# A four-layer graph network in float32: the second-last batch, too, mirrors a quarter of its symmetric products through VectorE and HBM, under a new instruction plan

## The chip, the cores and the metric

The kernel runs on one NeuronCore of a Trainium2 chip. The metric is the device time of one execution in microseconds (us). Before the change it is 2437.61 us, the median of three runs (2435.33 to 2437.78). The profile is that of one further execution, with a span of 2440.0 us.

The engines are named as in the profile: PE is TensorE's matrix multiplication and PEld its loading of weights, DVE is VectorE, ACT is ScalarE, POOL is GpSimd, SP is SyncE, from whose queue most transfers start.

## The reference, cut to what matters

There are 16 batches. Each has 1024 nodes with 128 features (`x`) and a 1024 x 1024 matrix of edge weights (`adj`), and passes four layers, each of the form x = x + layer(relu(layernorm(x))). All is float32. Two of the layers hold products that are symmetric in their two node indices, and the change is about these.

```python
# layer 0: three convolutions, each with a symmetric 1024 x 1024 product
def _adapt_conv(h, edge_weight, W, b, is_last):
    h = h @ W + b
    nh = h / jnp.maximum(jnp.linalg.norm(h, axis=-1, keepdims=True), EPS)
    cos = jnp.einsum('bij,bkj->bik', nh, nh)          # symmetric
    h = jnp.einsum('bpq,bqc->bpc', edge_weight * cos, h)
    return h if is_last else jax.nn.relu(h)

# layer 1: x_agg = adj^T x, then two dense layers         [cut]
# layer 2: attention over the edges, tanh and softmax     [cut]

# layer 3: one more symmetric product
    h = jnp.einsum('bnf,of->bno', x, W_w) + W_b
    e = jnp.einsum('bil,bkl->bik', h @ A, h)
    e = e + jnp.swapaxes(e, 1, 2)                       # symmetric
    att = jax.nn.softmax(jnp.where(adj > 0, e, 0), axis=1) * adj
    h_prime = jax.nn.relu(jnp.einsum('bij,bjk->bik', att, h))
    # ... gates and output                                [cut]
```

So a batch has four symmetric products: three in layer 0 and one in layer 3.

## The kernel before

The 1024 nodes are eight blocks of 128, so a product is an 8 x 8 grid of 128 x 128 blocks. It is made row by row (`j`), each row in two halves (`s`) of four blocks, that is 512 columns, one PSUM bank. Only the blocks on and above the diagonal are multiplied out (36 of 64). The 28 below it are mirrored from the blocks above, which are kept in SBUF in a buffer named `above`. There are two ways to mirror a block.

- **By TensorE.** ACT copies the blocks right of the diagonal from PSUM to `above`; later TensorE transposes each into the PSUM bank of its row.
- **By VectorE and HBM** (`by_dma`), for the lower left quarter only: rows 4 to 7, left half. VectorE transposes the right halves of rows 0 to 3 in squares of 32 x 32 as it takes them from PSUM to `above`; a transfer stores two rows of them to HBM, and four transfers bring them back with the squares in their mirrored places, into a buffer named `got`. VectorE then reads the half row from `got` in SBUF instead of from PSUM.

```python
def far(b, product):                       # which batches use VectorE and HBM
    return (b > 0 or "v" in FLAGS and product > 0) and b < (B - 1 if "u" in FLAGS else B - 2)

class Square:
    def row(self, j, s):
        lo, hi = HALVES[s]                                     # (0, 4), (4, 8)
        if self.by_dma and j >= QUARTER and s == 0:            # QUARTER is 4
            q = j - QUARTER
            return self.got, lambda: self.got.t.rearrange("p (r c d) -> p c r d", r=QUARTER, d=P)[:, q]
        dst = ps(f"sq_{self.k}_{j}_{s}")
        first = max(lo, j)
        if first < hi:
            pe(...)      # L761: one matmul of the blocks from the diagonal on
        n = min(hi, j) - lo
        if n > 0:
            pe(...)      # L771: n transposes of kept blocks, 128 x 128 each
        return dst, lambda: by_block(dst.t, D, 4)

    def keep(self, j, s, read):
        lo, hi = HALVES[s]
        if self.by_dma and j < QUARTER and s == 1:
            dve(...)     # L783: nc.vector.transpose of the four blocks, in squares
            if j % 2:
                self.send(j - 1, j + 1)    # L803 one store, L814 four loads
            return
        first = max(lo, j + 1)
        if first < hi:
            act(...)     # L793: nc.scalar.copy of the blocks right of the diagonal
    # [send() cut: one transfer above -> by_hbm, four by_hbm -> got]
```

Layer 0 uses a row like this, layer 3 in the same way with `e` and `hs` in place of `ew` and `h`:

```python
square = Square(k, hTn, hTn, "abc"[i] in FLAGS and far(b, i))
for j in range(NB):
    ew = chunk(f"ew_{k}_{j}")
    for s, (lo, hi) in enumerate(HALVES):
        pc, view = square.row(j, s)
        square.keep(j, s, pc)
        dve(...)         # L960: ew = (product * rn) * adjT, half a row
    accumulate(acc, h, j, D, ew, j)          # L823 (L834 in the last convolution)
```

With the flags of the kernel before, batches 1 to 13 mirror the quarter through HBM, and batches 0, 14 and 15 mirror all by TensorE.

The order of the instructions is not that of the program text. Each instruction is an `Op` with an assumed duration; `Plan.order()` lays all of them out on the engines in assumed time and then issues them in that order. Among the instructions that could start now, it takes the one of lowest rank:

```python
lead = self.leads.get(o.key + o.edge, self.leads.get(o.key, 0.0))
o.rank = (self.deadline(o.batch) - o.tail - lead, o.seq)
# deadline: lambda b: min(b * PERIOD, (B - 2) * PERIOD + LAST)
# o.tail: the longest chain of assumed durations behind it
```

`LEADS` has a number for each kind of instruction, with separate ones for the first two batches (`<0`, `<1`) and the last two (`>1`, `>0`). `KINDS` tells for each kind of buffer the pool, how many may be held at once, and how many by batches younger than the oldest in work. Two or three batches are in work at a time. The plan decides only order and buffers; the engines wait on semaphores as the data demand.

Of the kernel before, what the change touches and what calls it, by code (L numbers as in the profile page):

```python
# [222 lines left out]
def tile_adj_preln(  # L223
# [38 lines left out]
    hbm = ctx.enter_context(tc.tile_pool(name="hbm", bufs=1, space=bass.MemoryType.DRAM))  # L262
# [28 lines left out]
    FLAGS = set("CabcdkxhyzT")  # L291
# [34 lines left out]
    for load_it in first:  # L326
# [11 lines left out]
    POOLS = {"adjT": 16, "adjL": 5, "x": 3, "big": 13, "above": 2, "got": 1, "bank": 8, "small": 29, "row": 6, "hbm": 3, "hrow": 2}  # L338
    KINDS = {
        "adjT": ("adjT", 16, 16), "adjL": ("adjL", 5, 5), "x": ("x", 3, 3), "w4": ("big", 12, 8),  # L340
        "chunk": ("big", 11, 4), "above": ("above", 2, 1), "got": ("got", 1, 1), "ps": ("bank", 5, 5),
        "acc": ("bank", 8, 6), "small": ("small", 7, 6), "row": ("row", 3, 3), "hbm": ("hbm", 3, 2),
        "hrow": ("hrow", 2, 1),
    }
    PERIOD, LAST, AHEAD, WINDOW = 60.0, 52.0, 2, 0.05

    LEADS = {
        "0 ACT hT": -1, "0 DVE hn": -8, "0 DVE mv": 42.5, "0 DVE nb": -20, "0 DVE st": -77.5, "0 PE ps": -72.5,
        "0 POOL rstd": -1, "00 ACT above": -10.5, "00 ACT hT": 95, "00 ACT hTn": -20.5, "00 ACT sq": -31,
        "00 DMA by": -13.5, "00 DMA got": 15.5, "00 DVE above": -135, "00 DVE ew": 79.5, "00 DVE h": -95.5,  # L350
        "00 DVE ss": -131.5, "00 PE acc0": -252.5, "00 PE ps": -142, "00 PE psP": -0.5, "00 PE sq": -18.5,
        "00 POOL rn": -129.5, "01 ACT above": 56, "01 ACT hT": 11.5, "01 ACT hTn": 15, "01 ACT sq": 15.5,
        "01 DMA by": 4.5, "01 DMA got": 18.5, "01 DVE above": 4.5, "01 DVE ew": 51.5, "01 DVE h": -2.5,
        "01 DVE ss": 16, "01 PE acc0": -164.5, "01 PE ps": 42, "01 PE psP": -5.5, "01 PE sq": -11,
        "02 ACT above": -2, "02 ACT hTn": -615, "02 ACT sq": -25.5, "02 DMA by": 63.5, "02 DMA got": 0.5,
        "02 DVE above": 43.5, "02 DVE ew": -232.5, "02 DVE ss": 79.5, "02 DVE x": -55.5, "02 PE acc0": -28.5,
        "02 PE ps": 12.5, "02 PE sq": 222, "02 POOL rn": -103, "1 ACT g": -33, "1 ACT hn": 66, "1 ACT y1": -7.5,
        "1 DMA adjL": -113, "1 DVE adjL": -21, "1 DVE hn": 1.5, "1 DVE mv": 237.5, "1 DVE nb": 46,
        "1 DVE st": -625.5, "1 DVE x": -0.5, "1 PE acc1": 4, "1 PE py": -167.5, "1 PE py2": 67,
        "1 POOL rstd": -43, "2 ACT e2": -24, "2 ACT h": 287.5, "2 ACT hfl": 53, "2 ACT hn": -13.5,  # L360
        "2 ACT hnT": 18, "2 ACT s1": -14, "2 DVE alone": -51.5, "2 DVE e2": 48.5, "2 DVE h": 20,
        "2 DVE hn": 48.5, "2 DVE hrow": -43.5, "2 DVE mv": -2.5, "2 DVE nb": 78, "2 DVE rden": 9.5,
        "2 DVE x": 10, "2 PE acc2": 108.5, "2 PE p1": -90, "2 PE pf": -26.5, "2 PE ps": 117.5, "2 PE psP": -315,
        "2 POOL rstd": 4.5, "3 ACT above": -19.5, "3 ACT e3": 96.5, "3 ACT gate": -185.5, "3 ACT h3T": 19.5,
        "3 ACT hn": -84.5, "3 ACT hnT": -9.5, "3 ACT hp": -5, "3 ACT hpT": 41, "3 ACT hs": 46.5, "3 ACT z": 25,
        "3 DMA by": -13.5, "3 DMA got": 0.5, "3 DMA z": -130.5, "3 DVE e3": -363.5, "3 DVE gate": 83,
        "3 DVE h": -111.5, "3 DVE hn": 69, "3 DVE mv": -2, "3 DVE nb": 147, "3 DVE st": -192, "3 DVE sum": 53.5,
        "3 DVE top": -84, "3 DVE z": -925, "3 PE acc3": -130.5, "3 PE pg": -18.5, "3 PE ps": 19,
        "3 PE psN": 114, "3 PE psP": 95, "3 PE sq": -0.5, "3 POOL rstd": -59, "3 POOL z": 0.5,
        "T ACT adjT": 1.5, "T DMA adjT": -140.5, "T DVE adjT": -391, "x DMA x": 54.5, "0 ACT hT <0": -2,  # L370
        "0 ACT hT >1": -4.5, "0 ACT hn <1": -4.5, "0 DVE hn <0": 8.5, "0 DVE hn <1": 8.5, "0 DVE hn >0": 15.5,
        "0 DVE hn >1": 1, "0 DVE mv <0": -4.5, "0 DVE mv <1": 113, "0 DVE mv >0": 47.5, "0 DVE mv >1": -25.5,
        "0 DVE nb <0": 101.5, "0 DVE nb <1": -62.5, "0 DVE nb >0": -49, "0 DVE nb >1": -18.5,
        "0 DVE st <0": -85, "0 DVE st <1": -73.5, "0 DVE st >0": -122.5, "0 DVE st >1": -32, "0 PE ps <0": 85.5,
        "0 PE ps <1": 36, "0 PE ps >0": -31, "0 PE ps >1": 40, "0 POOL rstd <0": -6.5, "0 POOL rstd <1": -26,
        "0 POOL rstd >0": -7, "0 POOL rstd >1": 15.5, "00 ACT above <0": -32, "00 ACT above <1": -88,
        "00 ACT above >0": -294, "00 ACT above >1": -3, "00 ACT hT <0": 147.5, "00 ACT hT <1": -7,
        "00 ACT hT >0": 21, "00 ACT hT >1": 161.5, "00 ACT hTn <0": -70.5, "00 ACT hTn <1": 119.5,
        "00 ACT hTn >0": -22, "00 ACT hTn >1": -11, "00 ACT params <0": -26, "00 ACT sq <0": -34,
        "00 ACT sq <1": 134.5, "00 ACT sq >0": -119, "00 ACT sq >1": -25.5, "00 DMA by <1": 0,  # L380
        "00 DMA got <1": 1, "00 DVE above <1": -197, "00 DVE ew <0": 180, "00 DVE ew <1": 13,
        "00 DVE ew >0": -125, "00 DVE ew >1": -147.5, "00 DVE h <0": -25.5, "00 DVE h <1": -4.5,
        "00 DVE h >0": 12, "00 DVE h >1": -50.5, "00 DVE params <0": 171, "00 DVE ss <0": 0,
        "00 DVE ss <1": -73.5, "00 DVE ss >0": -46.5, "00 DVE ss >1": -4, "00 PE acc0 <0": -39.5,
        "00 PE acc0 <1": -212, "00 PE acc0 >0": -327.5, "00 PE acc0 >1": -253.5, "00 PE params <0": 56.5,
        "00 PE ps <0": -18.5, "00 PE ps <1": -16, "00 PE ps >0": -32, "00 PE ps >1": -130.5,
        "00 PE psP <0": -2.5, "00 PE psP <1": 32, "00 PE psP >0": -22.5, "00 PE psP >1": -43,
        "00 PE sq <0": 28.5, "00 PE sq <1": 10, "00 PE sq >0": 3.5, "00 PE sq >1": 10, "00 POOL rn <0": -11,
        "00 POOL rn <1": -164.5, "00 POOL rn >0": -96.5, "00 POOL rn >1": -144, "01 ACT above <0": 113,
        "01 ACT above <1": -11, "01 ACT above >0": 65.5, "01 ACT above >1": 24, "01 ACT hT <0": -15,  # L390
        "01 ACT hT <1": -17.5, "01 ACT hT >0": 3.5, "01 ACT hT >1": -39, "01 ACT hTn <0": 16.5,
        "01 ACT hTn <1": -22, "01 ACT hTn >0": 68, "01 ACT hTn >1": 8, "01 ACT sq <0": 174,
        "01 ACT sq <1": -3.5, "01 ACT sq >0": -69, "01 ACT sq >1": 107, "01 DMA by <1": -9, "01 DMA got <1": 25,
        "01 DVE above <1": -5, "01 DVE ew <0": 140, "01 DVE ew <1": -13.5, "01 DVE ew >0": -9.5,
# [983 lines left out]
    params = Buf(None, [], "params")  # L1378
# [57 lines left out]
```

## Time and profile before

| | before |
|---|---|
| time, median of three | 2437.61 us |
| span of the profiled execution | 2440.0 us |
| PE busy | 2389.2 us (98%) |
| DVE busy | 2106.2 us (86%) |
| ACT busy | 1288.3 us (53%) |
| POOL busy | 230.9 us (9%) |
| mean granted TensorE clock | 0.995 |
| HBM read, written | 198.14 MB, 62.91 MB |

Busy time is the time in which an engine executed at least one instruction; the shares are of the span. A float32 product appears in the records as two matmul records, a transpose by TensorE as one. Matmuls are pipelined: the recorded end of one lies behind the start of the next, so the distance from start to start is the better measure of what one costs. A line such as L771 is the place in the kernel that issued the instruction; the names beside it are the program's buffers, with the numbers left out (`sq<-ident,above` is a mirrored block, `got<-by_hbm` the load of squares). "Us to landing" of a transfer counts from its issue until its data are there.

### The profile page before, as it was taken

To read this page: it belongs to the slowest core of one execution; us is meant where nothing else is said; L and a number is where in the kernel's file an instruction comes from. 1 tells how busy PE (TensorE), PEld (TensorE's weight loads), DVE (VectorE), ACT (ScalarE), POOL (GpSimd) and SP (SyncE) were. 2 spreads that over 40 slices of the span, in tenths; PEclk is the share of its full clock that TensorE was granted. 3 is DMA by queue.
4 is the path that set the end of the run, shared out by engine and by line. 5 is a ranking of instruction groups with operands and counts; after the bars stand their busy time and mean duration, and the time that the engine had idled before them with its cause. 6 is when DMAs were issued, how large, how long until landed. Compare 5 with 4: busy or idle time off the path is not lost. (4 is left out here: it accounts for less than half of the span.)

```text
span 2440.0 us, 34840 instructions
## 1 busy us (share of the span) xinstructions
PE 2389.2 (98%) x11946; PEld 1588.9 (65%) x11946; DVE 2106.2 (86%) x5264; ACT 1288.3 (53%) x2404; POOL 230.9 (9%) x141
## 2 busy tenths in 40 slices
PE   6999999999999999999999999999999999999996
PEld 3568576675766757576575766757676575765763
DVE  5767989888998988999889998999989888897677
ACT  4425564644646455454644646455454655656275
POOL 1100010100101001011010100101011010101021
PEclk9999999999999999999999999999999999999999
DMA  8632837559296583946739296493946738054000
GB/s 127 131 96 43 147 78 139 126 93 178 54 160 132 85 158 78 159 109 114 160 75 182 58 153 134 87 162 68 162 116 105 164 78 156 18 87 95 25 2 18
DMA packets 1129473, 263.35 MB, mean 108 GB/s; under 512 B 971856, under 2 KB 1112912, under 8 KB 1129296
## 3 DMA queue, kind: packets, MB, share of 16 engines
q1 hardware_dynamic: 1108368, 251.73, 54.9%
q10 hardware_dynamic: 20928, 9.40, 1.4%
q8 instruction: 94, 1.54, 0.3%
q14 instruction: 83, 0.68, 0.1%
HBM read 198.14 MB, written 62.91 MB: 107 GB/s over the span
## 5 line engine op out<-in xcount | busy, mean ns | idle before, releaser
L960 DVE SCALAR_TENSOR_TENSOR ew<-sq,rn,adjT 128x512 f32<-128x512 f32 x612 | 432.0, 738 | 72.1 <-ACT above L793 37.4
L823 PE MATMUL acc<-ew,h 128*128 128x512 f32 x1024 | 481.5, 597 | 3.6 <-DVE ew L960 3.6
L761 PE MATMUL sq<-hTn 128*128 128x512 f32 (+3 forms) x1152 | 431.4, 487 | 0.3 <-ACT hTn L623 0.3
L793 ACT COPY above<-sq 128x256 f32<-128x256 f32 (+3 forms) x432 | 167.8, 393 | 439.0 <-PE sq L761 239.7
L761 PEld LDWEIGHTS sq<-hTn 128*128 128x128 f32 x1152 | 200.9, 191 | 153.2 <-issue 103.5
L823 PEld LDWEIGHTS acc<-ew,h 128*128 128x128 f32 x1024 | 179.8, 192 | 164.1 <-issue 124.1
L834 PEld LDWEIGHTS acc<-h,ew 128*128 128x128 f32 x2048 | 240.7, 192 | 23.0 <-issue 17.3
L834 PE MATMUL acc<-h,ew 128*128 128x128 f32 x2048 | 250.3, 276 | 0.0
L823 PE MATMUL acc<-e,hs 128*128 128x512 f32 x512 | 242.5, 598 | 5.6 <-DVE e L1203 4.4
L834 PEld LDWEIGHTS acc<-h,e 128*128 128x128 f32 x2048 | 232.9, 192 | 11.9 <-issue 6.5
L834 PE MATMUL acc<-h,e 128*128 128x129 f32 x2048 | 233.8, 275 | 1.2 <-DVE e L1110 1.2
L823 PE MATMUL acc<-adjL,hn 128*128 128x512 f32 x512 | 233.4, 593 | 0.3 <-ACT hn L727 0.3
L563 POOL TENSOR_TENSOR rstd<-ve,mhalf 128x8 f32<-128x8 f32 x64 | 105.1, 1642 | 1249.7 <-DVE ve L682 1197.6
L1194 ACT ACTIVATE e<-e,top 128x1024 f32<-128x1024 f32 x128 | 147.0, 1149 | 135.8 <-DVE top L1190 134.4
L771 PEld LDWEIGHTS sq<-ident,above 128*128 128x128 f32 x960 | 125.8, 141 | 135.4 <-issue 89.9
L891 ACT ACTIVATE adjT<-adjT 128x1024 f32<-128x1024 f32 x128 | 135.1, 1056 | 146.0 <-DVE adjT L888 109.4
L771 PE MATMUL sq<-ident,above 128*128 128x128 f32 x960 | 175.7, 274 | 9.7 <-ACT above L793 9.7
L888 DVE STREAM_TRANSPOSE adjT<-adjT 128x1024 f32<-128x1024 f32 x128 | 155.0, 1224 | 28.2 <-DMA adjT<-in_adj_dram 21.6
L706 ACT ACTIVATE hn<-x,nb,rstd 128x128 f32<-128x128 f32 x256 | 105.3, 483 | 123.6 <-DVE nb L690 117.8
L1110 DVE SCALAR_TENSOR_TENSOR e<-adjT,e 128x512 f32<-128x512 f32 x256 | 158.7, 679 | 9.3 <-ACT e L1106 8.8
L783 DVE STREAM_TRANSPOSE above<-sq 128x512 f32<-128x512 f32 x208 | 146.5, 706 | 17.2 <-PE sq L761 17.2
L1203 DVE TENSOR_TENSOR e<-e,adjT 128x512 f32<-128x512 f32 x248 | 161.0, 680 | 0.0
(130 smaller groups left out, 3493.8 us busy)
## 6 DMA issues: line engine op xcount, KB each, us to landing
adjT<-in_adj_dram SPq DMA_DIRECT2D x512, 128.0 KB, 4.0
adjL<-in_adj_dram SPq DMA_DIRECT2D x128, 512.0 KB, 5.2
by_hbm<-above SPq DMA_DIRECT2D x104, 512.0 KB, 4.0
got<-by_hbm SPq DMA_DIRECT2D x416, 128.0 KB, 3.8
x<-in_x_dram SPq DMA_DIRECT2D x15, 512.0 KB, 4.6
out_dram<-z ACTq DMA_DIRECT2D x15, 512.0 KB, 5.6
x<-in_x_dram SPq DMA_DIRECT2D x2, 256.0 KB, 5.1
out_dram<-z ACTq DMA_DIRECT2D x2, 256.0 KB, 2.3
```

Of the source, the lines that this page charges most:

```text
L761: lambda: nc.tensor.matmul(dst.t[:, (first - lo) * P :], cols(leftT.t, j), span(rightT.t, first, hi), start=True, stop=True),
L771: nc.tensor.transpose(cols(dst.t, r), cols(above.t, p), ident)
L783: lambda: nc.vector.transpose(span(above.t, p, p + 4), read.t),
L793: lambda: nc.scalar.copy(span(above.t, p, p + hi - first), read.t[:, (first - lo) * P :]),
L823: lambda s=s, lo=lo, hi=hi: nc.tensor.matmul(acc[s].t, cols(h.t, at, w), span(ew.t, lo, hi), start=(j == 0), stop=(j == NB - 1)),
L834: nc.tensor.matmul(a.t[:, (c - lo) * n : (c - lo + 1) * n], cols(ew.t, c), h.t[:, at * w : at * w + n], start=(j == 0 and c == lo), stop=( ...
L888: dve(V(N), [t], [t], lambda t=t: nc.vector.transpose(t.t, t.t), True)
L891: lambda t=t, c=c: nc.scalar.activation(t.t, t.t, AF.Copy, accum_out=su.t[:, c : c + 1]),
L960: lambda view=view, ew=ew, rn=rn, j=j, lo=lo, hi=hi: nc.vector.scalar_tensor_tensor(by_block(span(ew.t, lo, hi), D, 4), view(), rn.t[:, j ...
L1110: lambda e=e, j=j, lo=lo, hi=hi: nc.vector.scalar_tensor_tensor(span(e.t, lo, hi), span(aT[j].t, lo, hi), 0.0, span(e.t, lo, hi), op0=ALU. ...
L1194: lambda e=e, top=top, tot=tot: nc.scalar.activation(e.t[:, 0:N], e.t[:, 0:N], AF.Exp, bias=top.t, accum_out=tot.t),
L1203: lambda e=e, j=j, lo=lo, hi=hi: nc.vector.tensor_mul(span(e.t, lo, hi), span(e.t, lo, hi), span(aT[j].t, lo, hi)),
```

## The change

The change makes batch 14 mirror the lower left quarter of its four symmetric products through VectorE and HBM as well, so that only batches 0 and 15 mirror everything by TensorE. It is for taking these transposes off TensorE. As the set of instructions is then another one, the plan's numbers were found anew: all leads, the limits of the buffer kinds, the period and the offset of the last batch's deadline.

```diff
-    FLAGS = set("CabcdkxhyzT")
+    FLAGS = set("CabcdkxhyzTu")
...
-    POOLS = {... "bank": 8, "small": 29, "row": 6, "hbm": 3, "hrow": 2}
+    POOLS = {... "bank": 8, "small": 25, "row": 6, "hbm": 3, "hrow": 2}
     KINDS = {
-        "adjT": ("adjT", 16, 16), "adjL": ("adjL", 5, 5), "x": ("x", 3, 3), "w4": ("big", 12, 8),
-        "chunk": ("big", 11, 4), "above": ("above", 2, 1), "got": ("got", 1, 1), "ps": ("bank", 5, 5),
-        "acc": ("bank", 8, 6), "small": ("small", 7, 6), "row": ("row", 3, 3), "hbm": ("hbm", 3, 2),
+        "adjT": ("adjT", 16, 16), "adjL": ("adjL", 5, 5), "x": ("x", 3, 3), "w4": ("big", 12, 12),
+        "chunk": ("big", 9, 7), "above": ("above", 2, 1), "got": ("got", 1, 1), "ps": ("bank", 8, 7),
+        "acc": ("bank", 7, 4), "small": ("small", 12, 8), "row": ("row", 5, 4), "hbm": ("hbm", 3, 2),
         "hrow": ("hrow", 2, 1),
     }
-    PERIOD, LAST, AHEAD, WINDOW = 60.0, 52.0, 2, 0.05
+    PERIOD, LAST, AHEAD, WINDOW = 59.0, 22.0, 2, 0.05
 
     LEADS = {
     ... (all of its numbers replaced; in each version several hundred entries such as
-        "3 DVE z <0": -55, "3 DVE z <1": -68, "3 DVE z >0": 34.5,
+        "3 DVE z <0": -20.5, "3 DVE z <1": -50, "3 DVE z >0": -46, 
     ...)
```

## The prediction, made before the changed kernel ran

> **What bounds the kernel now.** I read the busy times first, then the windows of one fortieth of the span each, then TensorE's own waits. The first line gives each engine's busy time and its share of the 2440.0 us profiled:
>
> ```profile
> PE 2389.2 (98%) x11946; PEld 1588.9 (65%) x11946; DVE 2106.2 (86%) x5264; ACT 1288.3 (53%) x2404; POOL 230.9 (9%) x141
> ```
>
> TensorE is busy 98% and leaves 2440.0 − 2389.2 = 50.8 us. VectorE is next with 86%. Whether those 51 us lie in the loop or at the ends is told by the windows (start:end, length, then the busy time of PE, PEld, DVE, ACT and POOL; PEclk; DMA share; GB/s):
>
> ```profile
> 0.00:61.00 61.00, 40.11 (x156) 23.49 (x156) 35.81 (x98) 25.51 (x50) 7.29 (x10) 0.94 0.82 127
> 61.00:122.00 61.00, 57.63 (x231) 34.29 (x232) 45.97 (x95) 25.14 (x52) 6.51 (x4) 0.94 0.67 131
> ...
> 2074.00:2135.00 61.00, 61.00 (x352) 44.22 (x351) 51.32 (x162) 38.19 (x66) 6.51 (x4) 1.00 0.06 18
> 2135.00:2196.00 61.00, 61.00 (x318) 41.51 (x317) 57.12 (x111) 31.48 (x66) 3.27 (x2) 1.00 0.57 87
> ...
> 2318.00:2379.00 61.00, 58.27 (x328) 41.31 (x327) 46.56 (x115) 46.69 (x82) 12.33 (x6) 1.00 0.01 2
> 2379.00:2440.00 61.00, 41.48 (x160) 22.68 (x158) 42.97 (x112) 32.51 (x64) 11.87 (x6) 0.92 0.06 18
> ```
>
> The reader is to see that PE reads 61.00 of 61.00 in a window of the loop, while the first and the last windows hold the gaps: 61 − 40.11 = 20.9 and 3.4 us at the head, 2.7 and 19.5 us at the end. That is 46.5 of the 50.8 us; all 36 windows between share 4.2. The granted clock is 1.00 except at the two ends (0.94, 0.94 and 0.92). TensorE's own waits agree; the columns are who waited, for whom, total us, times, longest:
>
> ```profile
> PE ps_hT L570 <- DVE hn L699: 14.3, 2, 12.9
> PE sq L771 <- ACT above L793: 9.7, 6, 6.5
> PE acc L823 <- DVE e L1203: 4.4, 4, 2.0
> ```
>
> The rest of that list is under 4 us a row, and the first row is the start, where the first matmul stands at 12.92 us. At the end the trace has the last matmul finish at 2429.4 us, 10.6 us before the span's end. So 23.5 us of the 50.8 are a head and a tail in which TensorE has nothing yet or nothing more to do, and 27.3 us are waits between. Hence the first rule of this case: **an instruction taken off TensorE's queue before the last window shortens the kernel by its whole pace**, as long as nothing else takes over; an instruction taken off ACT, or a transfer added beside, moves nothing by itself.
>
> **What the Trainium skill says.** "Perfetto Trace Analysis", section "Identifying the Most-Contended Engine", says that matmul busy time is a poor measure because pipelined instructions overlap. The trace agrees: the mirrored transposes have a mean of 274 ns in the groups below, but four of them start only 0.44 us before the next instruction. I therefore count them by pace. "VectorE: DVE Perf Modes", section "The three transpose paths", says that VectorE transposes 32x32 blocks only, not a whole 128x128. That is why this path needs HBM at all: VectorE turns each square in place, and the transfers carry the squares to their places. "DMA: Bandwidth & Descriptors", section "Why small descriptors are slow (HBM only)", gives each packet a fixed overhead; the 32-float runs of these transfers are 128 B pieces. The trace agrees that pieces are small (971856 of 1129473 packets under 512 B) and shows what matters here, 3.8 us to landing. No run yet shows the packet overhead by itself.
>
> **The change, part by part.** The new flag makes the test for the HBM path true for batch 14 as well, in its four symmetric products (three of layer 0, one of layer 3). Batch 0 and batch 15 stay as they were.
>
> *Removed from TensorE.* In one product, rows 4 to 7 have their left half (four blocks) made by four transposes each: 16 transposes. Four products: 64 of the 960 there are now. (Check: batches 0, 14 and 15 make all 28 mirrored blocks of a product, 3 x 4 x 28 = 336; the 13 others make 12, 13 x 4 x 12 = 624; the sum is the 960 of the row.) The pace is read from the timeline of TensorE, where the columns are start, us, engine, line, operation:
>
> ```profile
> 2291.18 0.60 PE L771 MATMUL sq<-ident,above 128*128 128x128 f32 x4
> 2291.62 0.60 PE L761 MATMUL sq<-hTn 128*128 128x256 f32 x2
> ```
>
> Four transposes from 2291.18 to 2291.62: 0.44 us, 0.110 each. 64 x 0.110 = **7.0 us off TensorE**. The matmuls of the products themselves stay (36 blocks each either way).
>
> ```profile
> L771 PE MATMUL sq<-ident,above 128*128 128x128 f32 x960 | 175.7, 274 | 9.7 <-ACT above L793 9.7
> ...
> L783 DVE STREAM_TRANSPOSE above<-sq 128x512 f32<-128x512 f32 x208 | 146.5, 706 | 17.2 <-PE sq L761 17.2
> ```
>
> (The columns after the bar: busy us, mean ns of one, then idle before.) Counting with the group's 175.7 us / 960 = 0.183 us would give 11.7 us; I don't, because those ends overlap the next instruction.
>
> *Moved from ACT to VectorE.* Rows 0 to 3 of each product keep their right half. ACT copied it, as this row shows (48 = 3 batches x 16):
>
> ```profile
> L793 ACT COPY above<-sq 128x512 f32<-128x512 f32 x48 | 28.0, 586 | 25.1 <-PE sq L761 24.6 <-issue 0.2
> ```
>
> Sixteen go: 16 x 0.586 = 9.4 us off ACT, which is busy 53% and so gives nothing to the end. In their place stand 16 of the L783 transposes at 0.706: 11.3 us on VectorE. Where does it lie? By the starts of the product's matmuls (24 records to a product) the three products of batch 14's layer 0 begin at about 2023, 2091 and 2144 us, its layer 3 at 2336. In the windows shown for 2074 to 2196 VectorE is busy 51.32 and 57.12 of 61; two and a bit products' worth, about 12 x 0.706 = 8.5 us spread over 2013 to 2196, still fits, since the three windows there (53.66, 51.32, 57.12) leave 21 us. After 2318 it is busy 46.56 of 61, and 4 x 0.706 = 2.8 us fits. VectorE then reads these 16 halves from SBUF instead of PSUM at 745 against 738 ns and 679 against 671: nothing.
>
> *Added transfers.* Per product two stores and eight loads:
>
> ```profile
> by_hbm<-above SPq DMA_DIRECT2D x104, 512.0 KB, 4.0
> got<-by_hbm SPq DMA_DIRECT2D x416, 128.0 KB, 3.8
> ```
>
> Eight stores and 32 loads more, to 112 and 448. One round is 4.0 + 3.8 = about 8 us from the kept rows to use. In the window of 2074 to 2135 the DMA engines are at 0.06, in 2318 to 2379 at 0.01: the transfers have the queue to themselves. In the batches that do this already, VectorE waited for `got` 13.9 us in 13 waits over all 156 reads in layer 0, and that did not leave TensorE idle: its list of waits has no row that names it.
>
> *The new order.* Every lead, the limits of the buffer kinds, the period (60 to 59) and the offset of the last batch (52 to 22) change. The offset gives batch 15 a much earlier deadline beside batch 14, so more of batch 15's chain runs while batch 14 still fills TensorE. Nothing is added to any engine. It can win only out of the 27.3 us of waits: 11.3 us in the first two windows outside the 12.9 of the start, 4.2 in the loop, 11.7 in the last two outside the 10.6 of the tail. It can also lose there. I see no view that gives its size; I choose a net gain of 1 us.
>
> **Sum.** 2437.6 − 7.0 (transposes) − 1 (order) = 2429.6, rounded to **2430 us**, a ratio of 0.997.
>
> **The rivals.**
> 1. *The round through HBM shows up as a wait.* Batch 14's layer 3 runs late, at 2336, when only batch 15 is left to fill in. If rows 4 to 7 stand 8 us for `got` and batch 15 has nothing ready, the 1.76 us saved in that product turns into up to 6 us lost, and the kernel would take about 2436. For it: the scarcity of other work after 2318, where PE already shows 58.27 of 61. Against it: the right halves of rows 4 to 7 and the sums of rows 0 to 3 don't need `got`, and the DMA is idle.
> 2. *The end is set by VectorE's chain.* The chain that ended last is VectorE's in batch 15's layer 3 (DVE 1% of the span, PE 1%). If batch 15 cannot begin that chain earlier, the 7 us freed before become a hole ahead of it: about 2437, no change. For it: 19.5 us of idle TensorE in the last window. Against it: up to 2318 TensorE is full and everything of batch 15 stands behind it in the queue, so it moves up together.
> 3. *The order decides more than the transposes.* A better overlap of the last two batches could win up to the 11.7 us there: about 2418. A plan that stands worse on the chip than on paper (five or six waits of 2 us more in the first and last batches) would make 2442.
>
> **Range and chances.** The transposes' 7.0 us is the firm part; the ends may go about 12 us either way around 2430. So 2418 to 2442, 8 times in 10. Faster by over 2% means under 2388.9, that is 48.7 us: more than the 7.0 and the 27.3 us of waits together, so 1%. Slower by over 2% needs 49 us of new waits in a plan of the same kind as the old, which leaves 4.2 us idle in 36 windows: 2%.
>
> **What would show it.** The transposes of L771 at 896, the 512-wide copies of L793 at 32, the L783 transposes at 224, the loads of `got` at 448; PE's busy time about 7 us shorter or slightly more (its group counts overlap). TensorE at 61.00 in the windows of the loop. The first matmul near 12.9 us and the last one 10 to 11 us before the end. The prediction is wrong if TensorE's waits sum to over 60 us or under 40, if the list of its waits gains a row that leads back to `got`, or if VectorE's windows near 2100 go to 60 of 61 with TensorE no longer full there.

## The result and the profile after

The changed kernel takes **2456.08 us** (median of four, 2454.09 to 2458.19) against 2437.49 us for the kernel before. The ratio is 1.0078 with an interval of 1.0061 to 1.0096: 18.6 us slower, outside the predicted 2418 to 2442.

The first line of the page answers to the first line shown of before: PE, PEld, DVE, ACT and POOL, busy us, share of the span, instructions.

```profile
PE 2387.6 (97%) x11882; PEld 1584.6 (65%) x11882; DVE 2117.7 (86%) x5280; ACT 1270.9 (52%) x2388; POOL 230.5 (9%) x141
```

The instructions are what the diff says: 64 fewer on PE, 16 more on DVE, 16 fewer on ACT. The groups and the transfers confirm it by kind (after the bar: busy us, mean ns of one, then the idle time before the group; for transfers: count, KB, us to landing):

```profile
L778 PE MATMUL sq<-ident,above 128*128 128x128 f32 x896 | 165.6, 274 | 3.9 <-ACT above L800 3.9
L790 DVE STREAM_TRANSPOSE above<-sq 128x512 f32<-128x512 f32 x224 | 157.7, 708 | 35.1 <-PE sq L768 34.2
...
by_hbm<-above SPq DMA_DIRECT2D x112, 512.0 KB, 4.2
got<-by_hbm SPq DMA_DIRECT2D x448, 128.0 KB, 3.9
```

So the work is right and the time is not. The span profiled is 2452.3 us, and TensorE leaves 2452.3 − 2387.6 = 64.7 us idle instead of 50.8. Where do these lie? I split the span by stage and took the idle time of TensorE in each (the length of the stretch less PE's busy time):

| TensorE idle, us | 0–183 | 183–2013 | 2013–2200 | 2200–2330 | 2330–2380 | 2380–end | sum |
|---|---|---|---|---|---|---|---|
| before | 24.3 | 4.2 | 0 | 0 | 2.7 | 19.5 | 50.8 |
| after | 23.0 | 1.4 | 3.8 | 4.4 | 4.9 | 27.2 | 64.7 |

Up to 2013 us the new order is the better one by 4.1 us. From there on, where batches 13, 14 and 15 share the core, it loses 40.3 − 22.2 = 18.1: 8.2 us in 2013–2330, 7.9 us behind TensorE's last matmul (below), and only 2.0 us between 2330 us and that matmul (13.6 us idle against 11.7). The same stretches side by side, before first, show what moved (start:end, length, then busy time of PE, PEld, DVE, ACT and POOL; PEclk; DMA share; GB/s):

```profile
2100.00:2200.00 100.00, 100.00 (x568) 72.00 (x567) 87.92 (x192) 54.48 (x104) 6.54 (x4) 1.00 0.41 59
2200.00:2260.00 60.00, 60.00 (x241) 34.60 (x241) 44.39 (x122) 38.83 (x69) 5.18 (x3) 1.00 0.32 87
...
2365.00:2400.00 35.00, 32.46 (x184) 22.95 (x182) 23.47 (x68) 24.24 (x41) 14.52 (x7) 1.00 0.01 1
```

And after:

```profile
2100.00:2200.00 100.00, 97.47 (x468) 62.73 (x467) 92.03 (x182) 48.78 (x99) 6.82 (x4) 0.98 0.77 95
2200.00:2260.00 60.00, 60.00 (x249) 35.50 (x248) 31.83 (x95) 17.71 (x33) 3.95 (x3) 1.00 0.25 79
...
2365.00:2400.00 35.00, 30.51 (x114) 16.27 (x113) 33.28 (x57) 22.98 (x48) 5.04 (x2) 1.00 0.32 61
```

The third number after the length is VectorE. Its work has moved from 2200–2260 (44.39 to 31.83 us) to 2365–2400 (23.47 to 33.28 of 35): VectorE is nearly full there. Batch 14's layer 3 begins at 2362.7 us instead of 2335.9, and batch 15's at 2372.0 instead of 2392.9, so that the two run side by side. TensorE's own waits after the change (who, for whom, total us, times, longest):

```profile
PE acc L830 <- DVE ew L967: 6.4, 4, 3.0
PE acc L830 <- DVE e L1210: 6.0, 4, 2.7
PE acc L830 <- ACT hn L734: 4.8, 2, 4.4
```

Of these the 4.4 us stand alone in 2200–2330, and the waits for `e` in layer 3 after 2330. The row for `ew` is the head's: 6.2 of its 6.4 us lie before 183 us. There is no row that leads to `got`.

The end is another one, too. In the timeline of before (start, us, engine, line, operation) batch 14 is sent off first and the two halves of batch 15 last:

```profile
2400.00 0.38 ACTq L1314 DMA_DIRECT2D out_dram<-z  x1
...
2435.11 1.96 ACTq L1314 DMA_DIRECT2D out_dram<-z  x2
```

After the change (last column: idle before it) batch 15's second half is sent off at 2433.37, and then batch 14 still has its gated sums to do, on GpSimd:

```profile
2433.37 0.38 ACTq L1321 DMA_DIRECT2D out_dram<-z  x1
...
2435.32 1.91 POOL L1289 TENSOR_TENSOR hp<-hp,gate 128x1024 f32<-128x1024 f32 x1 [11.12 <-DVE gate L1303]
...
2445.73 2.34 POOL L1290 TENSOR_TENSOR z<-z,x 128x1024 f32<-128x1024 f32 x1
2448.09 0.38 ACTq L1321 DMA_DIRECT2D out_dram<-z  x1
```

From TensorE's last matmul to the end of the span it takes 18.5 us; before it took 10.6.

One caution for comparing spans: the execution of before that was profiled is about 4 us longer than its median and that of after 2 us shorter than its own, so the two spans differ by 12.3 us and the times by 18.6. Where it matters I count from the start of batch 11's output transfer, which leaves the head out: from there to the end it is 2440.0 − 1944.1 = 495.9 us before and 2452.3 − 1937.7 = 514.6 after. Of these 18.7 us more, 10.8 stand ahead of TensorE's last matmul and 7.9 behind it. The gain of the head is no accident of these two executions: in the seven profiles below that keep the old order, and in before's own, that transfer starts at 1942.4 to 1947.8 us, in the four of the new order at 1937.7 to 1940.9. Gain and loss together leave several us of the 18.6 to differences between executions that no profile shows.

### The profile page after: what moved, and what is told of

The parts are those of the page before. It is cut to its first block, busy times and chain, and to the rows that moved or that the text cites. A ratio compares the mean times of both kernels' runs of the same rounds, so it can differ in the third digit from the quotient of the medians.

```text
span 2452.3 us, 34785 instructions
## 1 busy us (share of the span) xinstructions
PE 2387.6 (97%) x11882; PEld 1584.6 (65%) x11882; DVE 2117.7 (86%) x5280; ACT 1270.9 (52%) x2388; POOL 230.5 (9%) x141
## 4 chain that ended last, share of the span: by engine, by line
PE 89%; DVE 5%; ACT 2%; DMA 2%; SPq 1%; issue 0%; POOL 0%; POOLq 0%; ACTq 0%; DVEq 0%
PE acc L830 34%; PE sq L768 19%; PE acc L841 17%; PE psP L608 5%; PE sq L778 4%; PE py L1029 2%; PE py L618 2%; PE ps_hTn L577 2%; PE ps_hnT L577 1%; PE pg L618 1%; DVE ew L967 1%; PE psN L608 1%; DVE e L1185 1%; DVE top L1197 1%; DMA got<-by_hbm 1%; PE ps_hT L577 1%
## 5 line engine op out<-in xcount | busy, mean ns | idle before, releaser
L967 DVE SCALAR_TENSOR_TENSOR ew<-sq,rn,adjT 128x512 f32<-128x512 f32 x600 | 422.1, 738 | 37.8 <-PE sq L768 14.3
L800 ACT COPY above<-sq 128x256 f32<-128x256 f32 (+3 forms) x416 | 159.0, 386 | 469.6 <-PE sq L768 253.5
L778 PEld LDWEIGHTS sq<-ident,above 128*128 128x128 f32 x896 | 118.6, 142 | 122.2 <-issue 92.3
L790 DVE STREAM_TRANSPOSE above<-sq 128x512 f32<-128x512 f32 x224 | 157.7, 708 | 35.1 <-PE sq L768 34.2
L895 DVE STREAM_TRANSPOSE adjT<-adjT 128x1024 f32<-128x1024 f32 x128 | 155.0, 1227 | 22.2 <-DMA adjT<-in_adj_dram 21.2
L778 PE MATMUL sq<-ident,above 128*128 128x128 f32 x896 | 165.6, 274 | 3.9 <-ACT above L800 3.9
```

The lines of the kernel that those rows point to most:

```text
L778: nc.tensor.transpose(cols(dst.t, r), cols(above.t, p), ident)
L790: lambda: nc.vector.transpose(span(above.t, p, p + 4), read.t),
L800: lambda: nc.scalar.copy(span(above.t, p, p + hi - first), read.t[:, (first - lo) * P :]),
L895: dve(V(N), [t], [t], lambda t=t: nc.vector.transpose(t.t, t.t), True)
L967: lambda view=view, ew=ew, rn=rn, j=j, lo=lo, hi=hi: nc.vector.scalar_tensor_tensor(by_block(span(ew.t, lo, hi), D, 4), view(), rn.t[:, j ...
```

## The experiments

Two theories stood at first. **The order**: the new numbers of the plan lose the time, and the path through HBM is not to blame. **The path**: VectorE's transposes or the round through HBM lose it. Times are medians; the ratio is to the kernel before on the same chip.

| kernel | time, us | ratio (95%) |
|---|---|---|
| new_numbers_no_path | 2460.0 | 1.0080 (1.0065–1.0095) |
| old_numbers_path | 2492.36 | 1.0216 (1.0200–1.0233) |
| old_order_path | 2482.94 | 1.0171 (1.0154–1.0188) |
| new_order_vector_end | 2456.58 | 1.0069 (1.0054–1.0084) |
| old_order_no_trip | 2450.28 | 1.0052 (1.0035–1.0068) |
| new_plan_last_two_again | 2445.89 | 1.0029 (1.0018–1.0041) |
| old_order_64_less | 2444.56 | 1.0023 (1.0014–1.0032) |
| new_order_no_trip | 2456.63 | 1.0076 (1.0062–1.0090) |
| new_order_64_less | 2457.76 | 1.0079 (1.0066–1.0091) |
| old_order_48_less | 2439.66 | 1.0006 (0.9998–1.0014) |
| old_order_read_sbuf | 2448.7 | 1.0042 (1.0028–1.0056) |
| old_order_read_sbuf_gpsimd_short | 2443.87 | 1.0019 (1.0013–1.0026) |
| old_order_gpsimd_short | 2439.5 | 1.0001 (0.9993–1.0009) |

### Either half of the change alone

**new_numbers_no_path** keeps all the new numbers and takes the path away; **old_numbers_path** keeps the old numbers and takes the path on. In both, the plan lays the instructions out once more, so each has an order of its own.

```diff
 new_numbers_no_path, against the kernel after
-    FLAGS = set("CabcdkxhyzTu")
+    FLAGS = set("CabcdkxhyzT")
 old_numbers_path, against the kernel before
-    FLAGS = set("CabcdkxhyzT")
+    FLAGS = set("CabcdkxhyzTu")
```

> The changed kernel with the one flag taken out again: batch 14 mirrors by TensorE as before, but all numbers of the plan are the new ones. Theory O (the order: the 18.6 us come from how the new plan lays the last two batches, whose layers 3 fall together so that batch 14 ends last) expects no recovery: 2450 to 2462 us, TensorE's idle time after 2013 us still near 40 us against 22 before. Theory P (the path: batch 14's trip through HBM and VectorE's 16 more transposes make TensorE wait) expects the loss to vanish: 2440 us or less.

> The kernel before with the one flag added and every number of the plan left as it was. The set of instructions is another one, so the same numbers give another order. Theory O expects slower than before by an amount that only the order sets, anything from 5 to 50 us, with the added time in gaps of TensorE in the last 400 us. Theory P expects about the loss of the change itself, 2450 to 2460 us, with gaps that lead back to got.

Without the path the new numbers are as slow as with it (1.0080 against 1.0078). With the path and the old numbers it is worse still, 2492 us. So the path can't stand under the old numbers, and the new numbers lose without the path. As neither order is that of a kernel being compared, the next runs hold an order fast.

### The new order with the path taken out piece by piece

**new_order_no_trip** has the order of the kernel after, instruction for instruction, without batch 14's eight stores and 32 loads; its sums read the kept squares where they lie. **new_order_64_less** also has ACT copy these halves, as before the change, in the places of VectorE's 16 transposes. Both leave out the mirroring of batch 14's quarter, so the values of that batch are others; only the time is read.

```diff
 new_order_no_trip, against the kernel after (stay is true for batch 14)
-                return self.got, lambda: self.got.t.rearrange(...)[:, q]
+                return self.got, lambda: (span(self.above.t, 6, 22) if stay else self.got.t).rearrange(...)[:, q]
...
-                lambda: nc.sync.dma_start(
+                lambda: None if stay else nc.sync.dma_start(
 new_order_64_less, on top of it
-                    lambda: nc.vector.transpose(span(above.t, p, p + 4), read.t),
+                    lambda: (nc.scalar.copy if self.k[:3] == "14_" else nc.vector.transpose)(span(above.t, p, p + 4), read.t),
```

> The changed kernel in its own order, with batch 14's transfers to HBM and back left out: its sums of rows 4 to 7 read the squares where VectorE put them (so batch 14's values are not the reference's). Theory O (the loss is the new order of the last two batches) expects the changed kernel's time again, within 4 us: 14 to 22 us over the kernel before. Theory T (the trip through HBM, which cost 33 us in the old order, costs here too) expects at least 10 us less than the changed kernel.

> The same without the trip, and with batch 14's half rows copied by ACT in place of VectorE's 16 transposes: of the whole path only the 64 transposes that TensorE doesn't do are left (batch 14's values are not the reference's). Theory O expects the loss to stand even so, at most 5 us under the changed kernel: 10 to 20 us over the kernel before. Theory L (VectorE's load of 11.3 us in the last batches) expects it back within 5 us of the kernel before.

2456.63 and 2457.76 us, ratios 1.0076 and 1.0079: the same loss as the whole change. In the new order neither the round through HBM nor VectorE's transposes cost anything beyond the 3 to 4 us of the intervals. The list of VectorE's waits of the kernel after says so as well; over all its batches it has

```profile
DVE ew L967 <- DMA got<-by_hbm: 12.0, 15, 1.5
```

against 13.9 us before. The whole loss is in the order of the instructions.

### The last two batches

**new_plan_last_two_again** is the kernel after, path and all, with 255 leads chosen anew, all of them of the last two batches (`>1` and `>0`), and LAST set to 42. The middle of the order stays nearly as it was.

```diff
-    PERIOD, LAST, AHEAD, WINDOW = 59.0, 22.0, 2, 0.05
+    PERIOD, LAST, AHEAD, WINDOW = 59.0, 42.0, 2, 0.05
...
+    LEADS.update({"0 ACT hT >0": -38.0, "0 ACT hT >1": 302.0, ... 255 entries, all ">0" or ">1"})
```

> The changed kernel, with the path through HBM for batch 14, the buffer limits and every lead of batches 0 to 13 as they are; only the leads of the last two batches and the offset of the last deadline (22 to 42) are chosen again, so that batch 15 ends last again, after batch 14, and through VectorE. Theory O (the loss is how the new plan lays the last two batches) expects most of the 18.6 us back: 4 us over to 8 us under the kernel before. Theory P (the path of batch 14 costs in any order) expects at least 10 us over the kernel before.

2445.89 us: 10 of the 18.6 us come back by the order of the last two batches alone. At 7 us over the kernel before, that lies between the two theories. Batch 15 is last again, and from the last matmul to the end it takes 10.8 us instead of 18.5. Counted from batch 11's output the rest of the run takes 2444.0 − 1939.0 = 505.0 us, against 514.6 and 495.9, so 7.7 of these 9.6 us are won behind the last matmul. The two layers 3 still run side by side (from 2364.4 and 2376.6 us): what this run takes back is the end, not that. It still doesn't reach the kernel before: TensorE is idle 4.1 and 4.4 us in 2013–2200 and 2200–2330, where before it was never idle.

**new_order_vector_end** tries the tail by itself: batch 14's gated sums, which end last, by VectorE instead of GpSimd.

```diff
-    pool_op(us, ..., lambda: nc.gpsimd.tensor_mul(part(a, w), part(a, w), per_node(of(g), n)))
-    pool_op(us + 0.4 * n / NB, ..., lambda: nc.gpsimd.tensor_add(part(z), part(a, w), part(c)))
+    for k in range(lo, hi):
+        s = gate.t[:, 3 * k + g : 3 * k + g + 1]
+        nc.vector.scalar_tensor_tensor(cols(z.t, k), cols(a.t, k, w), s, cols(c.t, k), op0=ALU.mult, op1=ALU.add)
```

> The changed kernel with its order kept, but the two gated sums of batch 14's finish, four GpSimd instructions of 1.9 to 2.4 us that stand at the very end, are done by VectorE in 16 of 0.34 us (0.26 from start to start). Theory O, which says that this batch ends last by GpSimd's chain, expects 4 to 6 us less than the changed kernel: 2450 to 2452 us. Theory P, which puts the loss into batch 14's waits for its squares, expects the end to move by under 2 us.

From the last matmul to the end it took 14.8 us instead of 18.5 in the profile, but the median stayed at 2456.58. The executions of this kernel spread over 5 us (2454.08 to 2459.16), more than the 3.7 us to be seen, so this run decides nothing about the tail.

### The old order with the path put in

**old_order_path** has the order of the kernel before, kept instruction for instruction: where ACT copied a right half of rows 0 to 3 of batch 14, VectorE now transposes it, the transfers go out right behind it, the 64 transposes of TensorE are left out, and the squares land in a buffer of their own, for which the pool of small buffers was cut from 29 to 24 (in every run of the old order but old_order_gpsimd_short; the cut was not measured by itself). **old_order_no_trip** leaves the transfers out and reads the kept squares. **old_order_64_less** also has ACT copy as before, so that only the 64 transposes are gone and the 16 sums read SBUF. **old_order_48_less** does that in layer 0 only. In the last three, batch 14's mirrored quarter holds other values.

```diff
 old_order_path, against the kernel before (swap: batch 14, rows 4 to 7, left half)
-                    for r, p in enumerate(at):
+                    for r, p in () if swap else enumerate(at):
...
+            if swap:
+                return dst, lambda: self.turned.rearrange(...)[:, j - QUARTER]
...
+                    if self.swap and j < QUARTER and s == 1:
+                        nc.vector.transpose(span(above.t, p, p + 4), read.t)
+                        if j % 2:
+                            self.send_now(j - 1, j + 1)      # a store, four loads
+                        return
 old_order_no_trip, on top of it
-                return dst, lambda: self.turned.rearrange(...)
+                return dst, lambda: span(self.above.t, 6, 22).rearrange(...)
-                        if j % 2:
-                            self.send_now(j - 1, j + 1)
 old_order_64_less, on top of it
-                        nc.vector.transpose(span(above.t, p, p + 4), read.t)
+                        nc.scalar.copy(span(above.t, p, p + 4), read.t)
 old_order_48_less, on top of it
-            self.swap = not by_dma and k in ("14_0", "14_1", "14_2", "14_3")
+            self.swap = not by_dma and k in ("14_0", "14_1", "14_2")
```

> The kernel before with its order kept instruction for instruction: only what stands at 16 places is exchanged (VectorE's transpose for ACT's copy, with the transfers right behind), batch 14's 64 transposes by TensorE are left out, and the squares land in a buffer of their own, so batch 13 and batch 14 share none. Theory O expects the transposes' 7.0 us to show, less a few us of stalls where VectorE is full: 2428 to 2437 us. Theory P expects 2450 us or more, with TensorE waiting behind got or behind VectorE near 2100 us.

> The same exchange in the old order that took 2482.94 us (against 2440.03 of the kernel before beside it), but without the ten transfers of each product: VectorE still transposes the 16 half rows, TensorE's 64 transposes are still left out, and the sums of rows 4 to 7 read the squares where they were kept, not moved to their mirrored places (so batch 14's values are not the reference's). Theory T (trip: in a fixed order the 43 us are VectorE standing in its queue until the squares have gone to HBM and back) expects all of it to vanish and the transposes' own worth to show: 7.0 us under the kernel before, within 3. Theory L (load: VectorE's 11.3 us more in a stretch where it is nearly full push everything behind) expects at least 10 us over the kernel before.

> The kernel before in its own order, with nothing changed but that batch 14's 64 transposes of the lower left quarters are left out: ACT copies the half rows as ever, no transfers are added, and the sums of rows 4 to 7 read the copies where they lie (so batch 14's values are not the reference's). Theory W (an instruction taken off the full TensorE is worth its pace) expects 7.0 us under the kernel before, within 2. Theory E (batch 15's own chain on VectorE sets the end, and the time saved becomes a hole ahead of it) expects 0 to 2 us under it.

> As old_order_64_less, but only for batch 14's three products of layer 0: 48 transposes are left out, and its layer 3 is that of the kernel before. In old_order_64_less the profile was 3.3 us ahead when layer 0 and batch 13 were done and lost it in layer 3, where two of the four sums that read SBUF took 2.8 us instead of 0.68 while GpSimd multiplied. Theory C (this collision on the way to SBUF, not the transposes, made that run slower) expects 3 to 5.3 us under the kernel before (5.3 is 48 x 0.110). Theory E (the last chain on VectorE sets the end and swallows what TensorE saves) expects 0 to 2 us under it.

Read from the top. With everything put in, the kernel is some 42 us slower (1.0171): in the old order the theory of the path is right. Without the transfers it is some 12 us slower (1.0052), so the round through HBM costs some 30 us in the order that was not made for it. VectorE's list of waits of old_order_path in 2013–2200, and TensorE in the same stretch:

```profile
DVE ew L982 <- DMA got<-by_hbm: 19.8, 3, 7.6
```

```profile
2013.00:2200.00 187.00, 163.03 (x772) 106.24 (x771) 144.10 (x351) 82.36 (x153) 13.76 (x8) 0.94 0.61 110
```

Three waits, the longest 7.6 us, about the 8 us of a store and a load; TensorE is idle 187 − 163.03 = 24 us where before it had no gap. With ACT's copies back as well the loss is 1.0023, so VectorE's 16 transposes account for about 1.0052 − 1.0023, 7 us (2 to 12 by the intervals). And with 64 transposes taken away, 7 us of TensorE by the prediction's pace, and 16 sums reading SBUF instead of PSUM, the kernel is **slower** by about 5 us (2444.56 against 2439.76 on the same chip). With 48 taken away it is within the interval of no change, 1.0006 (0.9998 to 1.0014), not 5.3 us faster.

The profile of old_order_48_less shows where most of the 5.3 us went. At 2122 us TensorE waits 0.71 us for VectorE's `ew`, where before it had no gap. Batch 14's layer 3 begins 388.4 us after batch 11's output instead of 391.8, that is 3.4 us earlier. This lead lasts until shortly before batch 15's layer 3, which TensorE's timelines show, before first (in brackets: idle before it, and for whom):

```profile
2386.07 1.66 PE L570 MATMUL ps_hnT<-ident,hn 128*128 128x128 f32 x8 [1.95 <-DVE hn L699]
...
2392.92 3.49 PE L761 MATMUL sq<-h3T,gT 128*128 128x512 f32 x8 [0.39 <-ACT h3T L623]
```

```profile
2381.08 1.81 PE L570 MATMUL ps_hnT<-ident,hn 128*128 128x128 f32 x8 [1.95 <-DVE hn L699]
...
2389.33 3.49 PE L763 MATMUL sq<-h3T,gT 128*128 128x512 f32 x8 [0.39 <-ACT h3T L623]
```

The gap is 1.95 us in both, but from its end to layer 3 it takes 8.25 us instead of 6.85. The windows behind the gap, before first, show why: the granted clock (PEclk, third number from the end) is 1.00 in one and 0.57 in the other.

```profile
2387.00:2391.00 4.00, 3.85 (x24) 2.76 (x23) 1.19 (x3) 2.52 (x5) 3.92 (x3) 1.00 0.01 2
```

```profile
2382.00:2386.00 4.00, 3.99 (x14) 2.58 (x13) 0.57 (x1) 1.84 (x4) 3.92 (x3) 0.57 0.01 2
```

From there 2.0 us are left, and they reach the end of the profile. What TensorE waits for in the last stage is the same, before first (after 2330 us):

```profile
PE acc L823 <- DVE e L1203: 4.1, 3, 2.0
```

```profile
PE acc L843 <- DVE e L1223: 4.1, 3, 2.0
```

So no hole opened ahead of the last chain: it moved up with the rest. The median of the times shows nothing of the 2.0 us, and that stays open.

### What made 64 slower than 48

The 16 transposes between the two are those of layer 3. There the four sums of rows 4 to 7 also changed from PSUM to SBUF. **old_order_read_sbuf** makes that one change and removes nothing: TensorE still does all transposes, and the four sums read half-row copies of the same shape in SBUF. Two more runs take GpSimd out of the stage: its four masking multiplies of batch 14's layer 3 cover 8 of 1024 columns, so that the rest of these rows stays unmasked, once with the reads from SBUF and once as a control.

```diff
 old_order_read_sbuf, against the kernel before (k == "14_3", rows 4 to 7, left half)
+            if swap:
+                return dst, lambda: span(self.above.t, 6, 22).rearrange(...)[:, j - QUARTER]
 old_order_read_sbuf_gpsimd_short on top of it, old_order_gpsimd_short on top of before
-    ... nc.gpsimd.tensor_mul(e.t[:, 0:N], e.t[:, 0:N], aT[j].t)
+    ... nc.gpsimd.tensor_mul(e.t[:, 0:8], e.t[:, 0:8], aT[j].t[:, 0:8])
```

> The kernel before in its own order with every transpose kept; only the four sums of batch 14's layer 3, rows 4 to 7, left half, read the copies in SBUF instead of the bank in PSUM (its values there are not the reference's). Nothing is added or taken away. Theory C expects two of these four instructions at 2.8 us instead of 0.68 and 4 to 5 us over the kernel before. Theory E expects no difference, within 1.5 us.

> As old_order_read_sbuf (order of before, nothing removed, only the left half of rows 4 to 7 of batch 14's layer 3 read from the kept copies in SBUF), but GpSimd's four masking multiplies of batch 14's layer 3 cover 8 of 1024 columns, so GpSimd is idle in that stage; batch 14's values are then not the reference's. Theory A (VectorE's SBUF-reading sum is stopped by the GpSimd multiply that runs at the same time): all four sums take about 0.68 us, and the time falls from 2448.7 to about 2438 to 2441. Rival B (the sums are slow, or the kernel is late, for another reason, such as two reads of SBUF colliding with ACT or the changed addresses): two sums still take 1.7 to 2.8 us and the time stays at about 2447 to 2449.

> The control: the kernel before with GpSimd's same four multiplies cut to 8 columns, everything else instruction for instruction the same. Both theories: GpSimd's own 2.4 us in four rows are off the way from the exponential to the row's products, so at most 1 to 3 us less than before, about 2435 to 2438. If it falls by as much as the run beside it falls under 2448.7, the gain there is GpSimd's own latency and not the end of a collision.

Reading SBUF instead of PSUM costs 10 us (2448.7, 1.0042), twice what the theory of a collision allowed. The timelines of VectorE and of GpSimd in that run show why (start, us, engine, line, operation, count):

```profile
2352.90 3.39 DVE L1198 SCALAR_TENSOR_TENSOR e<-adjT,above 128x512 f32<-128x512 f32 x2
...
2364.00 2.77 DVE L1198 SCALAR_TENSOR_TENSOR e<-adjT,above 128x512 f32<-128x512 f32 x1
...
2367.29 0.68 DVE L1198 SCALAR_TENSOR_TENSOR e<-adjT,above 128x512 f32<-128x512 f32 x1
```

```profile
2352.56 2.58 POOL L1219 TENSOR_TENSOR e<-e,adjT 128x1024 f32<-128x1024 f32 x1 [0.49 <-ACT e L1214]
2363.09 3.13 POOL L1219 TENSOR_TENSOR e<-e,adjT 128x1024 f32<-128x1024 f32 x1 [7.95 <-ACT e L1214]
```

The sum at 2364.00 takes 2.77 us instead of 0.68 and ends 0.55 us after GpSimd's multiply does (2363.09 + 3.13 = 2366.22); the pair at 2352.90 ends 1.15 us after the multiply that began at 2352.56. The Trainium skill says just this in "SBUF — State Buffer", section "Who interferes with whom": a VectorE instruction with two inputs in SBUF contends with a GpSimd instruction that reads SBUF, and the later one is blocked until the first is done. The prediction didn't draw on it. With GpSimd kept short the same four sums, in the group by shape, fall back from the first line to the second:

```profile
L1198 DVE SCALAR_TENSOR_TENSOR e<-adjT,above 128x512 f32<-128x512 f32 x4 | 6.8, 1729 | 0.0
```

```profile
L1198 DVE SCALAR_TENSOR_TENSOR e<-adjT,above 128x512 f32<-128x512 f32 x4 | 2.7, 690 | 0.0
```

and the time falls to 2443.87, ratio 1.0019, short of the 2438 to 2441 that the theory of a collision expected, while the control with the short multiply alone is where before is (1.0001). So the collision is about 1.0042 − 1.0019, 5.6 us (2 to 9 by the intervals), of the 10. The profiles agree: from batch 11's output to the end it takes 2446.9 − 1945.0 = 501.9 us with the reads from SBUF, 2438.4 − 1942.4 = 496.0 with GpSimd kept short too, and 495.9 before. The execution with 496.0 took 2440.2 us, 3.7 less than its median, and what the others spent more no profile caught. That rest of some 4 us stays open.

## Why the prediction was wrong

**Counts and costs of one: right; PE's busy time: wrong.** L778 is at 896, L790 at 224, the loads of `got` at 448; the means of L778 and L790 are within 1% of those used, the transfers' times to landing within 5%. Busy time of PE fell by 1.6 us instead of the 7.0. What makes up the difference is not separated: the clock is slower after 2013 us (below), but faster in the first 183 us (0.98 against 0.96). Two of the prediction's own signs came true: TensorE's idle time rose to 64.7 us, over 60, and the last matmul stands 18.5 us before the end instead of 10 to 11.

**The first rule: wrong, and the sum stands on it.** "An instruction taken off TensorE's queue before the last window shortens the kernel by its whole pace" was read from a 98% busy engine. In the old order 48 transposes less, 5.3 us by their pace, gave 3.4 us at batch 14's layer 3, 2.0 at the end of the profile and nothing that the times show. The 7.0 us was the firm part of the sum, and no run here shows it at the end. Full windows up to 2318 say that TensorE has no gap while these instructions are there; they don't say that none opens without them. One did, 0.71 us for VectorE, and behind a gap that was there already a slower clock took 1.4 us more. Rival 2 had the right size, no change, but its hole ahead of the last chain is not what the profile shows: that chain moved up.

**The new order as a gain of 1 us: the step that failed by most.** It was chosen without a view behind it, between 12 either way. Measured with the path taken out piece by piece, it is the whole loss of 18.6 us, and whatever the 64 transposes were worth on top. Rival 3 had the mechanism, "a plan that stands worse on the chip than on paper", with waits "in the first and last batches", but its 2442 is only 4 us over before. The head and middle were won, as hoped (4.1 us in the profile); from 2013 us on TensorE lost 18.1 us. The offset of the last batch, 52 to 22, was read as "more of batch 15's chain runs while batch 14 still fills TensorE". In the new plan batch 15's layer 3 did begin 21 us earlier, but batch 14's went back by 27 us, and batch 14 came last, through GpSimd: 7.9 us behind the last matmul. That this end is worth about that much is shown by the run that chose only the last two batches anew, which got 7.7 us of it back. With the two layers 3 side by side TensorE's waits in them grew by only 2.0 us. The gaps of 8.2 us in 2013–2330 stayed in every run of the new order; which numbers of the plan make them, and which of the 255 leads or the offset mended the end, is not separated.

**The transfers are hidden, the VectorE work fits: right in the new order, wrong in the old.** In the new order both cost nothing that shows (1.0076 and 1.0079 without them). In the old one the round costs about 30 us and the 16 transposes about 7. So Rival 1, the round as a wait, is real in the old order and worth far more than the 6 us given to it, and mostly in layer 0 (19.8 us in 2013–2200), not in layer 3 where the prediction looked (one wait of 4.1 us). The old order could not carry the path, and the one that came with it lost more than the path could bring. The 21 us of slack for VectorE were a sum over 183 us; they say nothing on whether the slack stands where the transposes come.

**Reading SBUF instead of PSUM: "nothing" was wrong** wherever GpSimd multiplies at the same time, for about 5.6 us in the old order. The mean of 679 ns, that of layer 3's sums from SBUF, came from batches in which GpSimd doesn't mask. In the kernel after none of these sums took over 0.69 us, batch 14's included: there they don't meet a multiply.

**Chances.** Same within 2% was the outcome, 0.97 as given; the range was too narrow on the slow side, because the new order was put at ±12 us without anything that limited it.

No version tried here beats the kernel before.

## What to carry to other kernels

An instruction taken off a full engine need not be worth its pace: without it another wait can open, and a gap further on can cost more than before. Of 5.3 us by pace 2.0 were left in a profile here and none in the times, so take such a saving as lost until a run shows it. When a change comes with a new order, the order is a change of its own, often the larger one: hold the order fast, take the new work out piece by piece, and look first at when each of the last pieces of work begins and which ends last. And before a read moves from PSUM to SBUF, look up what GpSimd is doing in that stage.

## What the runs showed of the hardware

**A gap on TensorE can be paid for twice.** I had counted gaps at their own length. In the kernel after, a stretch of half clock follows three of the gaps after 2013 us while TensorE has work, against one before. Its timeline of TensorE has four matmul records ahead of such a gap and seven behind it, of the same shape:

```profile
2157.96 1.88 PE L830 MATMUL acc<-e,hs 128*128 128x512 f32 x4
...
2167.25 5.13 PE L830 MATMUL acc<-e,hs 128*128 128x512 f32 x7 [1.91 <-ACT e L1201]
```

Four start 0.43 us apart (2157.96 to 2159.68), so seven should take about 3.2 us; they took 5.13. The windows around another gap, the 4.4 us before 2297, show the clock itself (PEclk, third number from the end):

```profile
2291.00:2297.00 6.00, 1.58 (x11) 1.11 (x10) 4.00 (x23) 5.85 (x11) 1.64 (x1) 1.00 0.00 0
2297.00:2300.50 3.50, 3.50 (x6) 1.54 (x5) 2.85 (x10) 3.50 (x6) 0.00 (x0) 0.55 0.05 8
```

Clock 0.55 over 3.5 us is 1.6 us of work lost. By estimate from these windows, three such stretches make some 4.5 to 5 us in the kernel after and one makes 1.3 in the kernel before, so about 3.5 us of what is lost after 2013 us are clock. In old_order_path the clock of the whole stretch 2013–2200 is 0.94: on 163 us of busy time that is, by estimate, about 10 us more, beside the 24 us of gaps. The Trainium skill has this in "TensorE: Matmul & The Clock Gate", section "What's actually happening": TensorE falls to half rate after an idle window of about 3.4 us and needs as long a busy one to come back. The half rate and the 3.4 us agree with the trace. The length of the gap doesn't quite: one of 1.91 us was enough at 2167, while one of 2.70 us at 2380 was not followed by it. Nor is it the length alone: the same gap of 1.95 us was followed by a slow stretch in old_order_48_less and not in the kernel before. In the clock records of these two traces and of after, all changes lie whole multiples of 3.413 us apart, so where a gap falls on that grid may decide; no run here tests it.

**VectorE is held up by GpSimd, not slowed.** A sum that takes 0.68 us took 2.77 beside a multiply on GpSimd when both of its large inputs lay in SBUF. Behind the multiply's end one sum needed 0.55 us more and a pair 1.15, about what they take alone (0.68 and 1.29), so they seem to have waited for the multiply rather than run slowly beside it. In the kernel before, with one of the two inputs in PSUM, three such sums in a row took 1.87 us together beside the same multiply:

```profile
2361.06 1.87 DVE L1178 SCALAR_TENSOR_TENSOR e<-adjT,sq 128x512 f32<-128x512 f32 x3
```

```profile
2361.08 2.38 POOL L1199 TENSOR_TENSOR e<-e,adjT 128x1024 f32<-128x1024 f32 x1 [6.86 <-ACT e L1194]
```
